# The column step of an inverse 2-D Haar transform: butterflies on VectorE in place of float32r products on TensorE

## The chip, the cores and the metric

The kernel runs on one core of one Trainium2 chip. The metric is the device time of one execution in microseconds; the time of a kernel is the median of its runs. The core's engines each run their own queue of instructions: TensorE (PE; PEld is its weight load), VectorE (DVE), ScalarE (ACT), GpSimd (POOL) and SyncE (SP), which here only issues transfers. PE writes its results to PSUM, which VectorE and ScalarE read.

## The reference

Four layers follow each other on an array of 4 batches, 64 channels and 256 x 256 points, in float32. Layers 0, 1 and 3 are separable 2-D convolutions, written as FFTs, with a residual. Layer 2 is the one in which the change lies: a 2-D Haar transform, two branches that scale the coefficients, mix the channels and shrink the result, and the inverse transform.

```python
def _L2_conv_ref(x, v, conv_w, tau):
    def haar1d_inv(x):
        n = x.shape[-1]
        length = 2
        for _ in range(int(np.log2(n))):
            half = length // 2
            a, d = (x[..., :half], x[..., half:length])
            inter = jnp.stack([NORM * (a + d), NORM * (a - d)], axis=-1)
            inter = inter.reshape(x.shape[:-1] + (length,))
            x = jnp.concatenate([inter, x[..., length:]], axis=-1)
            length *= 2
        return x
...
    f1 = haar2d(x)
    acc = jnp.zeros_like(f1[:, :conv_w.shape[1]])
    for i in range(v.shape[0]):
        f3 = f1 * v[i]
        f4 = jnp.einsum('bchw,oc->bohw', f3, conv_w[i])
        f5 = jnp.sign(f4) * jax.nn.relu(jnp.abs(f4) - tau[i])
        acc = acc + f5
    y = haar2d(acc, inverse=True)
    return y + x
```

Each level of the inverse turns a sum a and a difference d into a + d and a - d, so 8 levels rebuild 256 points from 256 coefficients. The output is layer 3 of this.

## The kernel before

A channel's 256 x 256 points lie as 128 partitions by 512. A convolution of a layer is a product with a Toeplitz matrix along each of the two axes (`contract`, L247 to L251: 128 x 128 weights, 256 and 128 columns, two of each for a product). The Toeplitz tiles are read from DRAM (`toeplitz`, L238). Each batch goes through three stages:

- **Convolutions of layers 0 and 1** (`convolutions`), a channel at a time: products a0, y0, a1, y1, each with a copy or a sum, then the forward Haar transform along the free axis (`pairs` and `levels`, on VectorE and GpSimd) and along the partitions (`down`, a product in two float32r halves). The coefficients go to DRAM as `coef`, and the sums and differences of the first level as `keep`.
- **Mixing** (`mixing`, L404 on), a group of four rows of all channels at a time, 64 groups: the channel product on PE (`mix`, L428), a scaling divided between VectorE (`scaled`, L447) and ScalarE (`scaled_too`, L452), `size` and `sign` on ScalarE (L456, L459), `shrink`, `signed` and `add` on VectorE (L463, L467, L471). `N_ACT` says how many of 16 columns ScalarE scales in each batch. `add` leaves the sum of both branches in the tile z, which holds a whole batch.
- **Inverse** (`inverse`, L491), a channel at a time. `butterfly` (L286, once a batch) makes the coarsest step of one axis. `fetch` loads r, the kept sums and differences, and copies the channel out of z on ScalarE (L501). `rows` (L504) makes one axis by a product with the Haar matrix and a transpose, into the PSUM tile pw. `halves` (L514) splits pw into a float32r part (a cast on ScalarE, L517) and the remainder (L518, VectorE). `cols` (L520) multiplies both halves with the matrix of signs hb, two products into the PSUM tile pu (L524). `join` (L529) adds half of r to pu (L532) and makes the last level (L535, L536), and the result u goes through layer 3: a3, a copy, y3, a sum (L281) and the store.

The order of the work is written out by hand. Every step is an event with a time in ticks, one channel or group per tick, with the offsets of the table `PLACE`; the events are sorted by time and run in that order. Batch b+1's convolutions are spread over batch b's mixing and the start of its inverse, so a mixing shares its ticks with convolutions and most of an inverse has none. In batches 0 to 2 every third channel (`put_off`) leaves layer 3 for later: its u is stored in `late`, and `convolution` takes it up during the last batch's mixing. From these events the build makes each engine's queue and all waits.

Buffers that the steps touch: PSUM tag "mm" has four one-bank tiles, shared by all products but the mixing's; "toep" has 5 tiles, "f" (r and the mixing's coefficients) 3, "mag" 2, "f4" 2, "y" (u among others) 3.

The rows of z are in the order of `_haar_order`, and the tables vt, taut and factors are laid out on the host to suit (`coefficients`, `kernel`).

Of the kernel before, what the change touches and what calls it, by code (L numbers as in the profile page):

```python
# [9 lines left out]
F32 = mybir.dt.float32  # L10
# [7 lines left out]
P = 128  # L18
# [31 lines left out]
    "shrink": 1.777,  # L50
    "signed": 2.802,
    "add": 3.331,
    "fetch": 0.414,
    "rows": 1.071,
    "halves": 1.522,
    "cols": 2.143,
    "join": 2.433,
    "aside": 3.357,
    "a3": 3.47,
    "a3 copy": 3.471,  # L60
    "y3": 4.542,
    "y3 sum": 4.542,
    "out": 5.537,
    "l load": 0.316,
    "l a3": 1.855,
    "l a3 copy": 1.855,
# [29 lines left out]
def conv_seq_kernel(ctx, tc, x, fz, fw, bias, decay, haar, haar_row, factors, vt, taut, wmix, out):  # L96
# [26 lines left out]


    hbt = const.tile([P, P], F32, name="hbt")
    hb = const.tile([P, P], F32R, name="hb")
    hbr = const.tile([P, P], F32R, name="hbr")
    hrow = const.tile([P, 2, P], F32, name="hrow")
    hsinv, ident = hrow[:, 0, :], hrow[:, 1, :]
# [1 line left out]
    bsb = const.tile([P, 3, C], F32, name="bsb")  # L131


    z = zpool.tile([P, 2, S, C], F32, name="z")

    sd = zpool.tile([P, 8, 2, 2, P], F32, name="sd")
    sums = zpool.tile([P, 4, 2, P], F32, name="sums")
# [6 lines left out]

    room = z.rearrange("p h r c -> p (h r c)")
    free = [0]

    def part(n, parts=P):  # L150
        free[0] += n
        return room[:parts, free[0] - n : free[0]]
# [53 lines left out]
        return [load, *steps, end, warm]  # L206

    def constants():
        signs = part(P)
        nc.sync.dma_start(hbt, haar[0])  # L210
        nc.sync.dma_start(signs, haar[1])
        nc.sync.dma_start(hrow, haar_row)
        nc.vector.memset(wb, 0.0)
        for r in range(2):
            nc.sync.dma_start(wb[r * C : (r + 1) * C, r, :], wmix)
        nc.scalar.copy(hb, signs)
        nc.scalar.copy(hbr, hbt)

    def tables():
# [63 lines left out]

        return [product, residual]

    def butterfly(b):  # L286

        d = mx.tile([P, 2, C], F32, name=f"bfly_{b}", tag="mag")
        nc.vector.tensor_sub(d, z[:, :, 0, :], z[:, :, 1, :])
        nc.vector.tensor_add(z[:, :, 0, :], z[:, :, 0, :], z[:, :, 1, :])  # L290
        nc.vector.tensor_copy(z[:, :, 1, :], d)  # L291

# [3 lines left out]
    def at(time, run, unit):  # L298
        events.append((time, len(events), run, unit))
# [104 lines left out]
    def mixing(b, start, n_act):  # L404

        st = {}

        def load(g):
            f = mx.tile([P, 2, S], F32, name=f"f_{b}_{g}", tag="f", bufs=3)
            nc.sync.dma_start(f, coef[b].rearrange("k c p w -> (k c) p w")[:, 2 * g : 2 * g + 2])  # L410
            st[g] = {"f": f}
            if g % GT == 0:
                t = mx.tile([P, 2, GT, 16], F32, name=f"vt_{b}_{g}", tag="vt")
                nc.sync.dma_start(t, scales[g // GT])
                st["vt", g // GT] = t

        def scale(g, i):
            return st["vt", g // GT][:, i, g % GT, :]

        def over(g, i, n):  # L420
            return scale(g, i)[:, :n].unsqueeze(2).to_broadcast([P, n, C])

        def mix(g):
            f = st[g]["f"]
            ps = psx.tile([P, 2, 2, S], F32, name=f"px_{b}_{g}", tag="mix")
            for q in range(2):
                for h in range(2):
                    nc.tensor.matmul(  # L428
                        ps[:, h, q, :],
                        f[:, q, h * P : (h + 1) * P],  # L430
                        wb.rearrange("p r n -> p (r n)"),
                        start=True,
                        stop=True,
                    )
            if g == 0:

                one, two = ps[:, :, 0, :P], ps[:, :, 0, P:]
                d = mx.tile([P, 2, P], F32, name=f"d_{b}", tag="mag")
                nc.vector.tensor_copy(d, two)
                nc.vector.tensor_sub(two, one, d)  # L440
                nc.vector.tensor_add(one, one, d)
            st[g]["f4"] = mx.tile([P, 16, C], F32, name=f"f4_{b}_{g}", tag="f4")
            st[g]["px"] = ps.rearrange("p h q (r i o) -> p (h q r i) o", r=2, i=2)

        def scaled(g):
            px, n = st[g]["px"], 16 - n_act
            nc.vector.tensor_tensor(st[g]["f4"][:, :n], px[:, :n], over(g, 0, n), ALU.mult)  # L447

        def scaled_too(g, half):
            px, f4 = st[g]["px"], st[g]["f4"]  # L450
            for j in range(16 - n_act + half * (n_act // 2), 16 - (1 - half) * (n_act - n_act // 2)):
                nc.scalar.mul(f4[:, j], px[:, j], scale(g, 0)[:, j : j + 1])  # L452

        def size(g):
            mag = st[g]["mag"] = mx.tile([P, 16, C], F32, name=f"mag_{b}_{g}", tag="mag")
            nc.scalar.activation(mag, st[g]["f4"], AF.Abs)  # L456

        def sign(g):
            nc.scalar.activation(st[g]["f4"], st[g]["f4"], AF.Sign)  # L459

        def shrink(g):
            mag = st[g]["mag"]
            nc.vector.tensor_sub(mag, mag, over(g, 1, 16))  # L463

        def signed(g):
            mag = st[g]["mag"]
            nc.vector.scalar_tensor_tensor(mag, mag, 0.0, st[g]["f4"], ALU.max, ALU.mult)  # L467

        def add(g):
            parts = st.pop(g)["mag"].rearrange("p (h r i) o -> p h r i o", h=2, i=2)  # L470
            nc.vector.tensor_add(z[:, :, 4 * g : 4 * g + 4, :], parts[:, :, :, 0, :], parts[:, :, :, 1, :])  # L471

        for g in range(S // 4):
            for name, stage in zip(
                ("mix load", "mix", "scaled", "scaled too", "scaled rest", "size", "sign", "shrink", "signed", "add"),
                (
                    load,
                    mix,
                    scaled,
                    lambda g: scaled_too(g, 0),  # L480
                    lambda g: scaled_too(g, 1),
                    size,
                    sign,
                    shrink,
                    signed,
                    add,
                ),
            ):
                at(start + g + PLACE[name if b + 1 < B else "l " + name], stage, g)

    def inverse(b, start, put_off):  # L491

        st = {}

        def fetch(c):
            if c == 0:
                butterfly(b)
            r = mx.tile([P, 2, 2, P], F32, name=f"r_{b}_{c}", tag="f", bufs=3)
            nc.sync.dma_start(r, keep[b][c])
            a = mx.tile([P, 2, 2, P], F32, name=f"zc_{b}_{c}", tag="mag")  # L500
            nc.scalar.copy(a, z[:, :, :, c].rearrange("p h (i k) -> p h k i", k=2))  # L501
            st[c] = {"r": r, "z": a}

        def rows(c):  # L504
            a = st[c]["z"]
            ps = psm.tile([P, 2, 2, P], F32, name=f"pw_{b}_{c}", tag="mm")
            for m in range(2):
                nc.tensor.matmul(ps[:, 0, m, :], a[:, 0, m, :], hsinv, start=True, stop=True)  # L508
                nc.tensor.transpose(ps[:, 1, m, :], a[:, 1, m, :], ident)  # L509
            st[c]["pw"] = ps  # L510
            if c not in put_off:
                st[c][2] = toeplitz(2, c, f"t2_{b}_{c}")

        def halves(c):  # L514
            w = st[c]["w"] = mx.tile([P, 2, 2, 2, P], F32R, name=f"w_{b}_{c}", tag="f4")
            ps = st[c]["pw"]
            nc.scalar.copy(w[:, 0], ps)  # L517
            nc.vector.tensor_tensor(w[:, 1], ps, w[:, 0].bitcast(F32), ALU.subtract)  # L518

        def cols(c):  # L520
            ps = psm.tile([P, 2, 2, P], F32, name=f"pu_{b}_{c}", tag="mm")
            flat = "p e m w -> p (e m w)"
            for i in range(2):
                nc.tensor.matmul(  # L524
                    ps.rearrange(flat), hb, st[c]["w"][:, i].rearrange(flat), start=(i == 0), stop=(i == 1)
                )
            st[c]["pu"] = ps

        def join(c):  # L529
            ps = st[c]["pu"]  # L530
            t = io.tile([P, 2, 2, P], F32, name=f"t_{b}_{c}", tag="res", bufs=BUFS["res"])
            nc.vector.scalar_tensor_tensor(t, st[c]["r"], 0.5, ps, ALU.mult, ALU.add)  # L532
            u = io.tile([P, 2, S], F32, name=f"u_{b}_{c}", tag="y", bufs=BUFS["y"])
            v = u.rearrange("p m (w e) -> p m w e", e=2)
            nc.vector.tensor_add(v[:, :, :, 0], t[:, 0], t[:, 1])  # L535
            nc.vector.tensor_sub(v[:, :, :, 1], t[:, 0], t[:, 1])  # L536
            st[c]["u"] = u

        def aside(c):
            nc.scalar.dma_start(late[b, c], st.pop(c)["u"])  # L540

        for c in range(C):
            for name, stage in zip(("fetch", "rows", "halves", "cols", "join"), (fetch, rows, halves, cols, join)):
                at(start + c + PLACE[name], stage, c)
            if c in put_off:
                at(start + c + PLACE["aside"], aside, c)
# [171 lines left out]
```

## Time and profile before

| | us |
|---|---|
| three runs | 2941.25 median, 2940.09 to 2941.63 |
| the profiled execution | 2941.06 |
| its span, first to last instruction | 2939.3 |

The granted clock of TensorE is full throughout. The four batches' mixings and inverses lie at 452 to 866 and 866 to 1079 us, 1079 to 1525 and 1525 to 1743, 1743 to 2189 and 2189 to 2403, 2403 to 2688 and 2688 to 2939; before 452 are the filters and batch 0's convolutions. The stage borders are the first and last instructions of `mix`, `add` and `butterfly` in the trace.

Instructions that the change touches, or whose like it adds (mean duration of one from start to write acknowledged; back-to-back instructions of VectorE overlap a little, so the sum of durations exceeds the busy time):

| line | engine, what | count | mean ns |
|---|---|---|---|
| L501 | ACT, copy of a channel out of z, 512 elements with a stride | 256 | 1104 |
| L508, L509 | PE, `rows` | 1024, 512 | 275, 273 |
| L517 | ACT, cast to float32r, 512 elements from PSUM | 256 | 587 |
| L372 | ACT, copy of 512 elements from PSUM | 256 | 683 |
| L532 | DVE, `join`, 512 elements | 256 | 686 |
| L535, L536 | DVE, `join`, 256 elements each | 512 | 418, 421 |
| L471 | DVE, `add`, 512 elements | 256 | 700 |
| L467 | DVE, scalar_tensor_tensor, 1024 elements | 256 | 1223 |
| L289, L290, L291 | DVE, `butterfly`, 128 elements | 4 each | 284, 289, 224 |

Transfers move 649.81 MB, 221 GB/s over the span. In an inverse they are r (256 KB a channel, 3.4 us from issue to landing), the Toeplitz tile of layer 3 (256 KB, 4.0 us) and the result (256 KB, 3.9 us).

To read the views: busy time is the union of an engine's instructions; ends of matmuls are modelled; the idle time in a group's row is that just before its instructions, with what ended it; the chain of waits is followed back from the last instruction and gives each piece the time until the next piece begins.

### The profile page before, as it was taken

The page shows a single profiled execution, that of the slowest core. Times are in us where ns is not written, and L with a number is a line of the kernel's source. Part 1 is how long each engine was busy: PE and PEld are TensorE (multiplying, and loading weights), DVE is VectorE, ACT ScalarE, POOL GpSimd, SP SyncE. Part 2 cuts the span into 40 slices and gives each one's busy share as a digit, 9 for nine tenths or more (in the row PEclk, how much of TensorE's full clock was granted, in tenths as well). Part 3 has the DMA queues.
Part 4 walks back from the last instruction along what each step waited for, and adds up shares of the span by engine and source line. Part 5 has one row for each costly group of instructions (what it writes and reads, how often), then busy time and mean ns, then how long its engine had stood idle before and what let it go on. Part 6 is the DMA issues. An engine that isn't in the chain of part 4 may idle for free. (4 is left out here: it accounts for less than half of the span.)

```text
span 2939.3 us, 52927 instructions
## 1 busy us (share of the span) xinstructions
PE 2894.3 (98%) x16950; PEld 2614.7 (89%) x16950; DVE 2397.6 (82%) x3931; ACT 2179.4 (74%) x5142; POOL 295.5 (10%) x644
## 2 busy tenths in 40 slices
PE   8999999999999999999999999999999999999999
PEld 6899998888888998999998998999998998888998
DVE  4655558988988878999888878999988889998776
ACT  2333348999986768999986768999986768887554
POOL 0111111211110001212110001212110000000000
PEclk9999999999999999999999999999999999999999
DMA  5877787776677876777777876777778878777766
GB/s 160 250 230 230 232 237 216 208 208 200 208 210 245 254 223 199 212 216 210 215 219 242 256 226 198 212 220 210 210 221 245 253 240 236 234 232 218 210 211 187
DMA packets 599368, 649.81 MB, mean 221 GB/s; under 512 B 48465, under 2 KB 517044, under 8 KB 598964
## 3 DMA queue, kind: packets, MB, share of 16 engines
q1 hardware_dynamic: 519860, 562.09, 65.7%
q10 hardware_dynamic: 79232, 84.34, 8.2%
q8 instruction: 137, 2.24, 0.3%
q14 instruction: 139, 1.14, 0.1%
HBM read 426.77 MB, written 219.48 MB: 220 GB/s over the span
## 5 line engine op out<-in xcount | busy, mean ns | idle before, releaser
L250 PE MATMUL py<-t,a 128*128 128x256 f32 x3072 | 920.0, 381 | 7.4 <-ACT a L264 7.0
L264 ACT COPY a<-pa 128x512 f32<-128x512 f32 x768 | 488.9, 637 | 375.2 <-PE pa L251 336.1
L452 ACT ACTIVATE f<-px,vt 128x64 f32<-128x64 f32 x2816 | 621.1, 401 | 94.6 <-DVE f L447 94.5
L251 PEld LDWEIGHTS py<-t,a 128*128 128x128 f32 x3072 | 583.6, 190 | 79.0
L251 PE MATMUL py<-t,a 128*128 128x128 f32 x3072 | 590.2, 274 | 0.0
L250 PEld LDWEIGHTS py<-t,a 128*128 128x128 f32 x3072 | 499.6, 191 | 50.6 <-ACT a L264 17.5
L428 PE MATMUL px<-wb,f 128*128 128x256 f32 x2048 | 489.5, 380 | 6.8 <-ACT f L452 6.7
L428 PEld LDWEIGHTS px<-wb,f 128*128 128x128 f32 x2048 | 369.0, 191 | 49.9 <-ACT f L452 10.0
L330 POOL TENSOR_TENSOR sd<-less 128x128 f32<-128x128 f32 (+4 forms) x320 | 160.3, 501 | 1929.6 <-DVE less L329 1884.5
L353 DVE TENSOR_TENSOR sp<-sd,sp 128x512 fp32r<-128x512 f32 x256 | 182.0, 711 | 184.4 <-ACT sp L348 183.9
L463 DVE TENSOR_TENSOR mag<-mag,vt 128x1024 f32<-128x1024 f32 x256 | 315.0, 1230 | 20.2 <-ACT mag L456 19.2
L467 DVE SCALAR_TENSOR_TENSOR mag<-mag,f 128x1024 f32<-128x1024 f32 x256 | 313.1, 1223 | 6.0 <-ACT f L459 3.8
L456 ACT ACTIVATE mag<-f 128x1024 f32<-128x1024 f32 x256 | 302.1, 1180 | 20.2 <-DVE z L471 19.6
L517 ACT CAST w<-pw 128x512 fp32r<-128x512 f32 x256 | 150.2, 587 | 223.7 <-PE pw L509 214.1
L250 PE MATMUL pa<-t,y 128*128 128x256 f32 x1024 | 307.6, 382 | 7.2 <-DVE y L281 4.1
L250 PE MATMUL pa<-t,x 128*128 128x256 f32 x1024 | 305.9, 381 | 0.4 <-DMA t<-pad 0.4
L459 ACT ACTIVATE f<-f 128x1024 f32<-128x1024 f32 x256 | 289.3, 1130 | 4.4 <-DVE y L281 1.2
L501 ACT COPY zc<-z 128x512 f32<-128x512 f32 x256 | 282.2, 1104 | 4.5 <-DVE z L291 1.4
L281 DVE SCALAR_TENSOR_TENSOR y<-y,bsb,py 128x512 f32<-128x512 f32 x256 | 190.3, 743 | 81.1 <-PE py L251 81.0
L250 PE MATMUL pa<-t,u 128*128 128x256 f32 x772 | 230.2, 380 | 5.3 <-issue 5.3
L532 DVE SCALAR_TENSOR_TENSOR t<-r,pu 128x512 f32<-128x512 f32 x256 | 175.6, 686 | 67.9 <-PE pu L524 64.1
L281 DVE SCALAR_TENSOR_TENSOR y<-x,bsb,py 128x512 f32<-128x512 f32 x256 | 190.3, 743 | 49.2 <-PE py L251 49.0
(72 smaller groups left out, 4636.9 us busy)
## 6 DMA issues: line engine op xcount, KB each, us to landing
t<-pad SPq DMA_DIRECT2D x768, 256.0 KB, 4.0
x<-in_x SPq DMA_DIRECT2D x256, 256.0 KB, 3.7
coef<-co SPq DMA_DIRECT2D x256, 256.0 KB, 3.0
f<-coef SPq DMA_DIRECT2D x256, 256.0 KB, 3.1
r<-keep SPq DMA_DIRECT2D x256, 256.0 KB, 3.4
out_y<-y ACTq DMA_DIRECT2D x256, 256.0 KB, 3.9
keep<-sums SPq DMA_DIRECT2D x256, 128.0 KB, 2.9
keep<-sd SPq DMA_DIRECT2D x256, 128.0 KB, 2.8
```

What stands on the lines that cost most here:

```text
L250: nc.tensor.matmul(ps[:, m, :], src[:, 0, m * P : (m + 1) * P], t[:, ::-1], start=True, stop=False)
L251: nc.tensor.matmul(ps[:, m, P:], src[:, 1, m * P : (m + 1) * P], t[:, : P - 1 : -1], start=False, stop=True)
L264: nc.scalar.copy(a, s["p" + new])
L281: nc.vector.scalar_tensor_tensor(y, s[res], bsb[:, layer, c : c + 1], s["p" + new], ALU.mult, ALU.add)
L353: nc.vector.tensor_tensor(w[:, 1], t, w[:, 0].bitcast(F32), ALU.subtract)
L428: nc.tensor.matmul(ps[:, h, q, :], f[:, q, h * P : (h + 1) * P], wb.rearrange("p r n -> p (r n)"), start=True, stop=True,)
L452: nc.scalar.mul(f4[:, j], px[:, j], scale(g, 0)[:, j : j + 1])
L456: nc.scalar.activation(mag, st[g]["f4"], AF.Abs)
L459: nc.scalar.activation(st[g]["f4"], st[g]["f4"], AF.Sign)
L463: nc.vector.tensor_sub(mag, mag, over(g, 1, 16))
L467: nc.vector.scalar_tensor_tensor(mag, mag, 0.0, st[g]["f4"], ALU.max, ALU.mult)
L501: nc.scalar.copy(a, z[:, :, :, c].rearrange("p h (i k) -> p h k i", k=2))
```

## The change

The levels of the column step are made in z itself, by butterflies on VectorE, before a channel is fetched; the float32r halves, the product with the signs and their tiles and constants go. The layout of z becomes [partition, chunk of 16 channels, row slot, 4, channel in chunk], so that a level of a chunk is one instruction over 64-element runs. `add` becomes two instructions, as the rows it writes go to the slots that in-place butterflies need (`place_of`), and `mix` writes its four results in another order of PSUM banks.

A level n of a chunk is a subtract and a scalar_tensor_tensor on 64n elements; level 32 is in two pieces and level 64 in four. They are placed as follows. Levels 1 to 32 of all four chunks, and level 64 of chunk 0, stand in the batch's own mixing, at ticks 12 to 15 (levels 1 to 8), 22 to 28 (16), 38 to 52 (32) and 43 to 66 (64). Level 64 of chunks 1 to 3 stands in the inverse, four pieces in the 16 ticks before the chunk is fetched. In the last batch all levels of chunks 1 to 3 stand there.

In the inverse `join` reads pw, one step after `rows`; all later steps come one tick sooner. r and the Toeplitz tile are loaded by a step of their own, `early`, ahead of `fetch`.

```diff
+    "early": -0.4,
     "fetch": 0.414,
     "rows": 1.071,
-    "halves": 1.522,
-    "cols": 2.143,
-    "join": 2.433,
-    "aside": 3.357,
-    "a3": 3.47,
...
+    "join": 1.433,
+    "aside": 2.357,
+    "a3": 2.47,
...
+    "level": 0.6,
...
-    z = zpool.tile([P, 2, S, C], F32, name="z")
+    z = zpool.tile([P, 4, P, 4, 16], F32, name="z")
...
+    def halve(even, odd):
+
+        nc.vector.tensor_sub(odd, even, odd)
+        nc.vector.scalar_tensor_tensor(even, even, 2.0, odd, ALU.mult, ALU.subtract)
+
+    def level(n, chunk, begin=0, count=None):
+
+        count = n if count is None else count
+        v = z.rearrange("p n s x c -> p n s (x c)")[:, chunk].rearrange("p (j e s) x -> p j e s x", e=2, s=P // 2 // n)
+        halve(v[:, begin : begin + count, 0, 0, :], v[:, begin : begin + count, 1, 0, :])
+
+    def butterfly():
+
+        v = z.rearrange("p n s (h k) c -> p n s h k c", k=2)
+        for h in range(2):
+            halve(v[:, :, 0, h, 0, :], v[:, :, 0, h, 1, :])
...
-                        ps[:, h, q, :],
+                        ps[:, q, h, :],
...
         def add(g):
-            parts = st.pop(g)["mag"].rearrange("p (h r i) o -> p h r i o", h=2, i=2)
-            nc.vector.tensor_add(z[:, :, 4 * g : 4 * g + 4, :], parts[:, :, :, 0, :], parts[:, :, :, 1, :])
+            parts = st.pop(g)["mag"].rearrange("p (q x i) (n c) -> p q i x n c", q=2, i=2, n=4)
+            for q in range(2):
+                slot = place_of(2 * g + q)
+                nc.vector.tensor_add(
+                    z[:, :, slot].rearrange("p n x c -> p x n c"), parts[:, q, 0], parts[:, q, 1]
+                )
...
+        def early(c):
             r = mx.tile([P, 2, 2, P], F32, name=f"r_{b}_{c}", tag="f", bufs=3)
             nc.sync.dma_start(r, keep[b][c])
+            st[c] = {"r": r}
+            if c not in put_off:
+                st[c][2] = toeplitz(2, c, f"t2_{b}_{c}")
+
+        def fetch(c):
             a = mx.tile([P, 2, 2, P], F32, name=f"zc_{b}_{c}", tag="mag")
-            nc.scalar.copy(a, z[:, :, :, c].rearrange("p h (i k) -> p h k i", k=2))
-            st[c] = {"r": r, "z": a}
+            nc.scalar.copy(a.rearrange("p h k i -> p (h k) i"), z[:, c // 16, :, :, c % 16].rearrange("p i x -> p x i"))
+            st[c]["z"] = a
...
-        def halves(c):
-            w = st[c]["w"] = mx.tile([P, 2, 2, 2, P], F32R, name=f"w_{b}_{c}", tag="f4")
+
+        def join(c):
             ps = st[c]["pw"]
-            nc.scalar.copy(w[:, 0], ps)
-            nc.vector.tensor_tensor(w[:, 1], ps, w[:, 0].bitcast(F32), ALU.subtract)
-
-        def cols(c):
-            ps = psm.tile([P, 2, 2, P], F32, name=f"pu_{b}_{c}", tag="mm")
-            flat = "p e m w -> p (e m w)"
-            for i in range(2):
-                nc.tensor.matmul(
-                    ps.rearrange(flat), hb, st[c]["w"][:, i].rearrange(flat), start=(i == 0), stop=(i == 1)
-                )
-            st[c]["pu"] = ps
-
-        def join(c):
-            ps = st[c]["pu"]
...
+        along = start - groups - 3
+
+        def when(tick, n, chunk, *span):
+            at(tick + PLACE["level"], lambda _: level(n, chunk, *span), 0)
+
+        at(along + 11 + PLACE["level"], lambda _: butterfly(), 0)
+        for chunk in range(4):
+            beside = b + 1 < B or chunk == 0
+            turn = start + 16 * (chunk - 1)
+            for n in (1, 2, 4, 8):
+                when(along + 12 + chunk if beside else turn, n, chunk)
+            when(along + 22 + 2 * chunk if beside else turn + 1, 16, chunk)
+            for i in range(2):
+                when(along + 38 + 4 * chunk + 2 * i if beside else turn + 2 + 2 * i, 32, chunk, 16 * i, 16)
+            for i in range(4):
+                when(turn + 4 + 3 * i if chunk else along + 43 + 8 * i - (i == 3), 64, chunk, 16 * i, 16)
```

## The prediction

> **What bounds the kernel now.** I read the busy table first, then the windows by stage, then the chain of waits, the cost groups and the timeline of one inverse.
>
> ```profile
> PE 2894.3 (98%) x16950; PEld 2614.7 (89%) x16950; DVE 2397.6 (82%) x3931; ACT 2179.4 (74%) x5142; POOL 295.5 (10%) x644
> ```
>
> TensorE is full over the whole span, but the room beside it differs by stage. The windows give span, then busy time of PE, PEld, DVE, ACT and POOL; in order, mixing and inverse of batch 0, of batch 1, and of batch 3 (batch 2 repeats batch 1):
>
> ```profile
> 452.00:866.00 414.00, 407.93 (x2248) 360.72 (x2247) 370.18 (x568) 406.77 (x1229) 75.79 (x130) 1.00 0.69 206
> 866.00:1079.00 213.00, 211.23 (x1350) 193.31 (x1350) 171.26 (x331) 140.24 (x199) 5.42 (x20) 1.00 0.79 242
> 1079.00:1525.00 446.00, 444.50 (x2508) 401.18 (x2507) 398.17 (x610) 399.00 (x1119) 76.15 (x140) 1.00 0.72 211
> 1525.00:1743.00 218.00, 216.23 (x1380) 197.92 (x1380) 174.19 (x336) 143.16 (x205) 5.27 (x20) 1.00 0.79 245
> ...
> 2403.00:2688.00 285.00, 277.01 (x1507) 247.51 (x1505) 278.30 (x330) 243.81 (x574) 0.00 (x0) 1.00 0.79 233
> 2688.00:2939.00 251.00, 246.66 (x1576) 227.35 (x1576) 175.61 (x324) 141.51 (x195) 0.00 (x0) 1.00 0.68 204
> ```
>
> The inverses are TensorE's alone. In the mixings VectorE is close behind (370 of 414, 398 of 446), and in the last one it is the bound: 278.3 of 285, 97.7%. So a microsecond saved on PE counts in the inverses, and one added to VectorE counts in the mixings.
>
> **What the change removes.** Two float32r products per channel (L524), the ScalarE cast (L517) and the VectorE remainder (L518).
>
> ```profile
> L524 PE MATMUL pu<-w,hb 128*128 128x512 f32 x512 | 181.4, 435 | 0.0
> L518 DVE TENSOR_TENSOR w<-pw,w 128x512 fp32r<-128x512 f32 x256 | 175.3, 685 | 2.5 <-ACT w L517 2.5
> L463 DVE TENSOR_TENSOR mag<-mag,vt 128x1024 f32<-128x1024 f32 x256 | 315.0, 1230 | 20.2 <-ACT mag L456 19.2
> ```
>
> The chain of waits (start, length, what) prices them better, because it counts each step only until the next begins:
>
> ```profile
> 2854.11 0.46 PE pu L524 x2
> ...
> 2632.28 1.13 DVE mag L463
> 2633.93 1.22 DVE mag L467
> ```
>
> The pair of products holds the path for 0.46 us: 256 x 0.465 = 119 us, about 30 in each inverse. The Trainium skill, Perfetto Trace Analysis, section Identifying the Most-Contended Engine, calls matmul busy time a bad measure because matmuls are pipelined. The busy row would make the gain 181 us and the end 62 us lower than the chain does; the chain agrees with the page, so the chain is used.
>
> On ScalarE 37.5 us go from each inverse, where it has 70 us free: worth nothing. On VectorE L518 goes: 64 x 0.60 (its start to L535's in the timeline below) = 38.5 us per inverse.
>
> **What it adds to VectorE.** A butterfly is a subtract and a scalar_tensor_tensor that waits for it. Level n of a chunk is 64n elements: 64, 128, 256, 512, then 1024 once, twice and four times. For 1024 elements the chain shows 1.13 followed by independent work and 1.22 followed by a wait: 2.35 a pair, 7 pairs a chunk, 16.5 us. The small levels by rows: 0.69 (L518), 0.42 (L535), 0.28 (L289), and about 0.22 for 64 elements, which no row has (an estimate, 0.28 less half the step from 0.42); twice their sum is 3.2. A chunk is 19.7 us, 16 of them 315 us. `add` becomes two instructions of 256 elements, 0.33 apart, for one of 512 at 0.60: +0.07 x 64 = 4.5 us per mixing. The old butterfly (three instructions, 0.8 us) and the new (four) cancel.
>
> The Trainium skill, VectorE: DVE Perf Modes, section The DRAIN you can't avoid, speaks against the change: the next instruction starts only when the pipe is empty, and chained ones gain nothing. The rows show an independent successor starting 0.1 us before the reported end (1.13 against 1.23). By the rule a pair would be 2.46 and all levels 12 us dearer; the rows are used.
>
> By stage, in us of VectorE: mixing 0 to 2 get levels 1 to 32 of four chunks, 4 x (3.2 + 3 x 2.35) = 41.0, level 64 of chunk 0, 9.4, and 4.5: **+55 each**. Mixing 3 gets one chunk and 4.5: **+24**. Inverses 0 to 2: -38.5 + 12 x 2.35 = **-10**. Inverse 3: -38.5 + 59 = **+21**.
>
> **Where that lands.** Mixing demand becomes 425, 453, 453 and 302 us. If every idle moment were used the stages grow by 11, 7, 7 and 17, together 42; if the added work overlapped nothing, by 189. The nearest row is mixing 3, which VectorE bounds at 97.7%; dividing by that gives 435, 464, 464 and 309: +21, +18, +18, +24 = **+81**, which I take.
>
> The inverses lose 119 on PE and must hand some back, because VectorE's levels come between steps that PE needs. Its queue there, batch 3:
>
> ```profile
> 2748.67 0.75 DVE L281 SCALAR_TENSOR_TENSOR y<-u,bsb,py 128x512 f32<-128x512 f32 x1 [0.66 <-PE py L251]
> 2749.80 0.69 DVE L532 SCALAR_TENSOR_TENSOR t<-r,pu 128x512 f32<-128x512 f32 x1 [0.38 <-PE pu L524]
> 2750.41 0.68 DVE L518 TENSOR_TENSOR w<-pw,w 128x512 fp32r<-128x512 f32 x1
> 2751.01 0.42 DVE L535 TENSOR_TENSOR u<-t 128x256 f32<-128x256 f32 x1
> 2751.34 0.42 DVE L536 TENSOR_TENSOR u<-t 128x256 f32<-128x256 f32 x1
> 2752.42 0.75 DVE L281 SCALAR_TENSOR_TENSOR y<-u,bsb,py 128x512 f32<-128x512 f32 x1 [0.66 <-PE py L251]
> ```
>
> A tick is 3.74 us and becomes 3.28: a3 1.31, y3 1.31, rows 0.66. VectorE does the y3 sum (0.66) and `join` (about 1.39 with its wait) and idles 1.2 us, room for one 1024-element instruction per tick. Written in the order of the code, a pair of 2.35 stands between a y3 sum and the `join` behind it, and a3 waits for that `join`. It has 3.94 us (rows, a3, y3, rows) for 2.25, so a pair makes PE 0.8 late; the five crowded ticks at a chunk's start cost about 6, the three later pairs 2.4, some 9 us a chunk, 28 for batch 3. In batches 0 to 2 every third channel is put off, three ticks take PE 7.2 and the window is 2.63 us: 2.1 late per pair in chunks 1 and 3, about 0.8 in chunk 2, 20 per batch. That is the upper end, 88; the lower is 0.
>
> The queue is not the order of the code, though: L518 stands between the instructions of one `join` above, and the cast of `constants`, placed at tick 4.93 (about 42 us by the `pairs` instructions, which place tick 4.64 at 40.4), ran at once:
>
> ```profile
> L217 ACT CAST hbr<-hbt x1: 298/298/298, 8.2 to 8.2; 128x128 fp32r<-128x128 f32 x1
> ```
>
> So the build moves ready work forward into idle time, and levels are ready long before they are due. I take three tenths of the upper end: 6, 6, 6 and 8, **+26**.
>
> **At nothing**, with cover: `early` issues r 0.8 and the t2 load 1.5 ticks sooner on SP; r's third-last buffer is free 1.2 ticks before, so nothing behind it (coefficient, x and filter loads) waits; if it were not, `join` would be late by part of a 3.4 us landing. PSUM has one allocation per channel less. The channel copy (L501, 1.10 us) reads with another stride; between 0.68 (L372) and 2.2 (twice its row) ScalarE stays under 175 of 183 us. The new bank order of `mix` lets L447 start up to 0.43 us sooner; VectorE waits for px 9.5 us in mixing 0, so 0 to -9.5; I take 0. DMA moves the same bytes in about 189 instead of 213 us: 242 GB/s becomes 273, which single slices of 4 us in the inverse of batch 0 exceed:
>
> ```profile
> GB/s 256 190 267 219 312 226 253 311 212 311 192 310 244 245 258 224 250 277 281 229 284 207 326 266 228 259 221 261 242 268 212 273 217 236 262 251 259 226 242 243
> ```
>
> **Sum**, on the profiled execution (2941.06 us: span 2939.3 and 1.8 around it; the runs' median is 2941.25, the same): 2941 - 119 + 81 + 26 = **2929 us**.
>
> **Rivals.** (1) VectorE's idle takes it all: +42 in the mixings, nothing handed back: 2864; with half of each expected loss, about 2885. For it: levels wait for nobody and fit any gap. Against: three engines at 98% in mixing 0 have never run without waits. Chance 0.18. (2) Slower: the level pairs stand where the code puts them, between the y3 sum and `join`, and PE waits at a3: +88 in the inverses, 2941 - 119 + 81 + 88 = 2991. It decides from 38 us handed back. For it: VectorE's own work per chunk in inverse 3 (16 x 2.05 + 19.7 = 52.5) equals PE's (16 x 3.28 = 52.5). Against: the moved instructions above. Chance 0.33. (3) The change doesn't do what it says because the transfers hold the first three inverses at their length: -22 from inverse 3 and +81 give 3000. For it: DMA is busy 0.79 there already; against: the slices at 310 GB/s. Chance 0.05.
>
> **How the numbers follow.** The forecast has 0.44, its own range 2905 to 2947. A measurement here tells about 0.2% from no change, 2935.4 to 2947.1. Faster is 0.30 of the forecast's 0.44 and rival 1: 0.48; same 0.10; slower 0.04 of the forecast and rivals 2 and 3: 0.42. The range 2880 to 3005 leaves out nearly half of rival 1 and the far parts of rivals 2 and 3, together 0.2.
>
> **What would show it.** Mixings of 435, 464, 464 and 309 us with VectorE at 97%; inverses of about 190, 194, 190 and 229 us, each with some 6 us in which a3 waits for `join`; L524's 119 us gone from PE. If the first mixing stays below 425 the levels were cheaper than 2.35 a pair; if PE shows over 15 us of waits for `join` in an inverse, rival 2 holds; if r lands late, rival 3.

## The result, and the profile after

| | before | after |
|---|---|---|
| median of five runs, us | 2941.25 | 2954.99 |
| lowest to highest | 2939.57 to 2941.98 | 2952.87 to 2959.32 |
| profiled span, us | 2939.3 | 2957.5 |

The ratio is 1.0049, 95% interval 1.0034 to 1.0064: the changed kernel is slower by half a per cent, more than the 0.2% that a measurement here can tell. The forecast was 2929 us, faster. It missed by 26 us and had the wrong sign. The profiled execution is the slowest of the five.

The busy table of the kernel after:

```profile
PE 2826.3 (96%) x16438; PEld 2541.0 (86%) x16438; DVE 2529.3 (86%) x4287; ACT 2056.6 (70%) x4885; POOL 361.2 (12%) x644
```

The 512 products are gone (16950 to 16438) and the butterflies are there: VectorE is busy 132 us longer. Yet the span is 18 us longer, and TensorE, full before, now stands idle. The windows by stage of the kernel after say where (span, then busy time of PE, PEld, DVE, ACT, POOL, the granted clock, the DMA share and GB/s); mixing and inverse of batches 0, 1 and 3:

```profile
451.00:884.00 433.00, 418.26 (x2284) 367.20 (x2283) 421.53 (x709) 410.11 (x1233) 80.84 (x130) 1.00 0.67 200
884.00:1096.00 212.00, 188.99 (x1194) 172.22 (x1193) 158.45 (x288) 108.76 (x133) 12.90 (x20) 0.96 0.77 242
1096.00:1550.00 454.00, 452.25 (x2544) 407.19 (x2543) 443.36 (x741) 398.34 (x1121) 95.23 (x140) 1.00 0.71 209
1550.00:1767.00 217.00, 196.06 (x1221) 177.76 (x1220) 162.06 (x295) 111.57 (x138) 12.71 (x20) 0.95 0.78 242
...
2429.00:2733.00 304.00, 285.28 (x1517) 250.94 (x1515) 300.00 (x422) 248.02 (x575) 0.00 (x0) 0.99 0.74 220
2733.00:2957.00 224.00, 216.35 (x1432) 200.94 (x1432) 185.07 (x318) 108.39 (x129) 0.00 (x0) 1.00 0.75 224
```

With the stage borders put at the first product of `mix` and the first copy of `fetch` in both traces:

| stage | before | after | difference | predicted |
|---|---|---|---|---|
| mixings 0 to 3 | 415.6, 447.8, 447.8, 287.2 | 433.3, 454.0, 453.9, 303.9 | +18, +6, +6, +17 | +21, +18, +18, +24 |
| inverses 0 to 2 | 211.1, 217.0, 211.9 | 211.9, 216.8, 208.5 | +1, 0, -3 | -24 each |
| inverse 3 | 250.9 | 224.3 | -27 | -22 |

The mixings grew less than predicted and inverse 3 shrank more. But inverses 0 to 2 lost 30 us of products each and are as long as before: all of the error is there. TensorE is busy 189 of 212 us in inverse 0, against 211 of 213 before.

Cut into its start, its middle and its end, inverse 0 of the kernel after (the same view):

```profile
884.00:932.00 48.00, 37.62 (x199) 33.41 (x198) 45.29 (x69) 16.37 (x23) 12.54 (x18) 0.86 0.56 170
932.00:1024.00 92.00, 81.14 (x520) 73.28 (x520) 61.15 (x118) 52.48 (x66) 0.36 (x3) 0.98 0.80 250
1024.00:1096.00 72.00, 70.23 (x478) 65.53 (x478) 52.01 (x103) 39.91 (x46) 0.00 (x0) 1.00 0.89 280
```

There are two places, and they differ. In the first 48 us VectorE is full (45.3) and TensorE idles 10 us. In the next 92 VectorE has 31 us free and TensorE still idles 11. At the end nothing waits, and the transfers run at 280 GB/s.

The start, on VectorE and then on TensorE (the timeline of the kernel after: start, length, line, operation, shape, and in brackets the idle time before it and what ended it). Lines are numbered as in the changed kernel: L284 and L285 are the two instructions of a pair of a level, L533, L536 and L537 are `join`, L246 and L247 the products of `contract`, L277 the sum behind a y product, and L322, L323 and L359 belong to the next batch's convolutions.

```profile
889.94 1.21 DVE L284 TENSOR_TENSOR z<-z 128x1024 f32<-128x1024 f32 x1
891.08 0.41 DVE L322 TENSOR_TENSOR sums<-y 128x256 f32<-128x256 f32 x1
891.41 0.42 DVE L323 TENSOR_TENSOR sd<-y 128x256 f32<-128x256 f32 x1
891.75 1.21 DVE L285 SCALAR_TENSOR_TENSOR z<-z 128x1024 f32<-128x1024 f32 x1
892.89 0.68 DVE L533 SCALAR_TENSOR_TENSOR t<-r,pw 128x512 f32<-128x512 f32 x1
895.11 0.69 DVE L359 TENSOR_TENSOR sp<-sd,sp 128x512 fp32r<-128x512 f32 x1 [1.55 <-ACT sp L354]
895.72 0.42 DVE L536 TENSOR_TENSOR u<-t 128x256 f32<-128x256 f32 x1
896.06 0.42 DVE L537 TENSOR_TENSOR u<-t 128x256 f32<-128x256 f32 x1
```

```profile
893.78 0.38 PE L247 MATMUL py<-t,a 128*128 128x128 f32 x2
896.53 0.73 PE L246 MATMUL pa<-t,u 128*128 128x256 f32 x2 [2.37 <-DVE u L537]
```

Levels stand here that the code places as late as tick 45 of the inverse: the build moved them forward, as it moved the cast of `constants`, and all 12 pairs of level 64 of chunks 1 to 3 are done by 931 us, when channel 6 has just come to `join`. One `join` is drawn out over 3.6 us, because work of the next batch's last convolutions (L359, which waits 1.55 us for ScalarE) stands in it, and a3 waits 2.37 us.

The middle holds no level at all. What the y3 sums waited for there (the view of one line, idle time of its engine and what ended it):

```profile
L277 DVE SCALAR_TENSOR_TENSOR y<-u,bsb,py x38: 737/747/749, 907.0 to 1076.9; 128x512 f32<-128x512 f32 x38
...
  PE py L247: 22.9, 17
  DMA coef<-co: 8.6, 6
```

And one such wait, on VectorE:

```profile
961.06 0.69 DVE L533 SCALAR_TENSOR_TENSOR t<-r,pw 128x512 f32<-128x512 f32 x1
963.12 0.75 DVE L277 SCALAR_TENSOR_TENSOR y<-u,bsb,py 128x512 f32<-128x512 f32 x1 [1.37 <-DMA coef<-co]
963.78 0.42 DVE L536 TENSOR_TENSOR u<-t 128x256 f32<-128x256 f32 x1
964.12 0.42 DVE L537 TENSOR_TENSOR u<-t 128x256 f32<-128x256 f32 x1
```

```profile
964.64 0.67 PE L246 MATMUL pa<-t,u 128*128 128x256 f32 x2 [1.35 <-issue]
```

The sum writes into a tile of tag "co", of which there are two. The coefficient copies of the next batch's last convolutions (L378) use the same two, and a tile is free only when its store has landed, 3.2 us (coefficients) or 3.8 us (results) after its issue. So the sum waits for a store, VectorE's queue stands behind it, `join` is late, and a3 begins 0.1 us after `join` ends.

### The profile page after: what moved, and what is told of

Same layout as the page of the kernel before. It is cut to its first block, busy times and chain, and to the rows that moved or that the text cites. A ratio compares the mean times of both kernels' runs of the same rounds, so it can differ in the third digit from the quotient of the medians.

```text
span 2957.5 us, 52078 instructions
## 1 busy us (share of the span) xinstructions
PE 2826.3 (96%) x16438; PEld 2541.0 (86%) x16438; DVE 2529.3 (86%) x4287; ACT 2056.6 (70%) x4885; POOL 361.2 (12%) x644
## 5 line engine op out<-in xcount | busy, mean ns | idle before, releaser
L246 PE MATMUL py<-t,a 128*128 128x256 f32 x3072 | 927.7, 384 | 8.8 <-ACT a L260 8.3
L247 PEld LDWEIGHTS py<-t,a 128*128 128x128 f32 x3072 | 587.6, 191 | 81.3
L247 PE MATMUL py<-t,a 128*128 128x128 f32 x3072 | 593.3, 275 | 0.0
L246 PEld LDWEIGHTS py<-t,a 128*128 128x128 f32 x3072 | 498.2, 193 | 48.3 <-ACT a L260 19.6
L336 POOL TENSOR_TENSOR sd<-less 128x128 f32<-128x128 f32 (+4 forms) x320 | 200.8, 627 | 1899.8 <-DVE less L335 1644.8
L246 PE MATMUL pa<-t,y 128*128 128x256 f32 x1024 | 310.3, 385 | 16.6 <-DVE y L277 10.0
L246 PE MATMUL pa<-t,x 128*128 128x256 f32 x1024 | 305.8, 380 | 0.9 <-issue 0.9
L246 PE MATMUL pa<-t,u 128*128 128x256 f32 x772 | 241.0, 395 | 61.4 <-issue 42.6
L359 DVE TENSOR_TENSOR sp<-sd,sp 128x512 fp32r<-128x512 f32 x256 | 178.1, 696 | 128.0 <-ACT sp L354 126.5
L277 DVE SCALAR_TENSOR_TENSOR y<-u,bsb,py 128x512 f32<-128x512 f32 x193 | 143.7, 745 | 144.9 <-PE py L247 108.9
L277 DVE SCALAR_TENSOR_TENSOR y<-x,bsb,py 128x512 f32<-128x512 f32 x256 | 189.3, 740 | 46.7 <-PE py L247 45.7
L247 PEld LDWEIGHTS pa<-t,y 128*128 128x128 f32 x1024 | 195.6, 191 | 26.8
L247 PEld LDWEIGHTS pa<-t,x 128*128 128x128 f32 x1024 | 194.6, 190 | 26.3
```

The lines of the kernel that those rows point to most:

```text
L246: nc.tensor.matmul(ps[:, m, :], src[:, 0, m * P : (m + 1) * P], t[:, ::-1], start=True, stop=False)
L247: nc.tensor.matmul(ps[:, m, P:], src[:, 1, m * P : (m + 1) * P], t[:, : P - 1 : -1], start=False, stop=True)
L277: nc.vector.scalar_tensor_tensor(y, s[res], bsb[:, layer, c : c + 1], s["p" + new], ALU.mult, ALU.add)
L336: engine.tensor_tensor(t[:, :, :, half:length], v[..., 0], v[..., 1], ALU.subtract)
```

## The experiments

All twelve are variants of the changed kernel, but for one of the kernel before. Ratios are to the kernel before on the same chip; its medians on the chips used lie within 2.3 us of each other.

**Four kernels: buffers against levels.** Theory: the "co" buffers hold the middle, the level instructions the start. Rival: it is the levels alone, as rival 2 had it.

Four "co" buffers in place of two:

```diff
-BUFS = {"res": 1, "y": 3, "co": 2}
+BUFS = {"res": 1, "y": 3, "co": 4}
```

> The changed kernel with four buffers for the tag co (the results of layer 3 and the coefficients) instead of two; 2954.99 us with two. Theory (the y3 sum waits for a buffer whose store has not landed, holds VectorE's queue, and with it join and a3): from channel 6 to 36 of inverses 0 to 2 a tick falls from about 3.1 us to 2.55, some 16 us a batch; in all about 2907 us, and the waits of the y3 sum on a transfer are gone. Rival one (the transfers of these stretches are too slow): no change, within 5 us. Rival two (the Haar levels on VectorE make the waits): no change in those channels, since no level runs there.

Measured: 2917.06 us, ratio 0.9908 [0.9893, 0.9923]. This one number turns the loss into a gain of 0.9%. Its y3 sums (the same view of one line) wait for no transfer any more:

```profile
L277 DVE SCALAR_TENSOR_TENSOR y<-u,bsb,py x41: 734/745/750, 907.5 to 1077.2; 128x512 f32<-128x512 f32 x41
...
  PE py L247: 22.9, 20
  ACT a L260: 1.2, 1
```

Inverses 0 to 2 take 198.0, 199.8 and 196.5 us; the other stages moved by less than 1 us. Start, middle and end of inverse 0:

```profile
885.00:933.00 48.00, 38.55 (x208) 34.03 (x206) 45.49 (x69) 16.93 (x23) 12.92 (x20) 0.86 0.56 173
933.00:1024.00 91.00, 89.33 (x590) 81.88 (x591) 69.39 (x137) 59.68 (x74) 0.00 (x0) 1.00 0.93 287
1024.00:1083.00 59.00, 58.17 (x398) 54.59 (x397) 42.15 (x83) 31.92 (x37) 0.00 (x0) 1.00 0.92 286
```

TensorE is full in the middle; the start is as it was. The gain is 10 us short of the 2907 expected.

The kernel before with four buffers, as a control:

> The kernel before with four buffers for co. Theory: its inverse has waits of 1.9 us on PE in all, so the buffer costs it nothing: 2941 us, within 4. Rival (more buffers help any kernel of this layout): 2 us or more faster per batch, below 2933 us.

Measured: 2943.08 us, ratio 0.9999 [0.999, 1.0008]. Two buffers were enough at its tick of 3.0 us in the middle of these inverses; they are not at the 2.65 us to which the tick falls with four.

Level 64 of chunks 1 to 3 left out in batches 0 to 2:

```diff
-            for i in range(4):
+            for i in range(4 if b + 1 == B or chunk == 0 else 0):
```

> The changed kernel without level 64 of chunks 1 to 3 in batches 0 to 2 (24 instructions of 1024 elements per batch left out), two buffers for co. Theory of the buffer: only the first 48 us of each of the three inverses get shorter, by 10 to 15 us a batch, and channels 6 to 36 stay at about 3.1 us a tick: 2910 to 2925 us. Rival (the levels are all of it): the 30 us of waits in each inverse go, about 2860 us.

Measured: 2925.40 us, ratio 0.9936 [0.992, 0.9952], just above what was expected. `join` of channel 12 comes 6 to 12 us sooner, counted from the first fetch copy; channels 12 to 36 still take 3.1 to 3.2 us each on average, against 3.1 to 3.3 with these levels. So these levels are not what holds the middle.

All levels left out:

```diff
-        nc.vector.tensor_sub(odd, even, odd)
-        nc.vector.scalar_tensor_tensor(even, even, 2.0, odd, ALU.mult, ALU.subtract)
+        return
```

> The changed kernel without any level and without butterfly (all added VectorE work except the second add left out). Theory: the mixings return to 414, 448, 448 and 287 us (48 us less), the starts of the inverses lose 12 us each and inverse 3 some 5; channels 6 to 36 keep their 3.1 us a tick. About 2955 - 48 - 41 = 2866 us. Rival (the levels are all of it): PE's 119 us come out whole, 2941 - 119 = 2822 us.

Measured: 2887.23 us, ratio 0.9799 [0.978, 0.9819], above both expectations. The middle of inverse 0 in this kernel:

```profile
932.00:1024.00 92.00, 80.73 (x521) 73.58 (x522) 61.25 (x120) 51.26 (x62) 0.00 (x0) 0.98 0.80 246
```

Without any level TensorE loses the same 11 of 92 us there. In the middle rival 2 falls and the buffers stand.

**Four more: how many buffers, what the levels cost, and what the build's order is worth.** Three buffers:

> The changed kernel with three buffers for co (two: 2954.99 us, four: 2917.06). Theory: a y3 sum comes some 2 to 2.4 us behind the last one where no channel is put off between, and a coefficient tile takes a buffer for about 5 us (copy 0.7, store 3.9) every fourth tick; with three buffers the third-last store has had 5 us or more, so nearly all of the wait goes: 2917 to 2925 us. Rival (what counts is the room for coefficients of several channels at once): halfway, about 2936 us.

Measured: 2915.41 us, ratio 0.9908 [0.9893, 0.9923]: the third buffer does it all, the fourth nothing.

No levels and four buffers:

> Four buffers for co and no levels and no butterfly (left out). Theory: the two causes stand at different places (channels 6 to 36 against mixings and starts of inverses) and add up: 2917 less the 68 us that leaving out the levels brought with two buffers, 2849 us. Rival (they wait for the same thing): above 2865 us.

Measured: 2841.95 us, ratio 0.9658 [0.9642, 0.9674], 7 below. This closes a table of medians in us:

| | levels | no levels | levels cost |
|---|---|---|---|
| two co buffers | 2955.0 | 2887.2 | 68 |
| four co buffers | 2917.1 | 2842.0 | 75 |
| two instead of four cost | 38 | 45 | |

The two costs are almost independent. And 2842 is 20 above 2941 - 119 = 2822: with neither cost, a sixth of the gain on TensorE still doesn't arrive. The start of inverse 0 in this kernel, and the whole of it:

```profile
883.00:931.00 48.00, 45.23 (x296) 41.25 (x295) 34.70 (x69) 26.38 (x33) 2.85 (x10) 1.00 0.86 262
866.00:1056.00 190.00, 185.00 (x1224) 170.39 (x1223) 139.41 (x272) 110.72 (x137) 5.87 (x20) 1.00 0.90 275
```

Without levels TensorE is busy 45.2 us of these 48, against 38.6 with four buffers and the levels: in inverse 0 the levels hold the start.

The pairs of level 64 held back to the tick where the code has them, by a one-element multiply on ScalarE that each pair must wait for (four buffers):

```diff
+        def hold(c, chunk, begin):
+            odd = z[:, chunk, 2 * begin + 1, 0, 0:1]
+            nc.scalar.mul(junk, odd, st[c]["z"][:, 0, 0, 0:1])
...
+                if chunk and b + 1 < B:
+                    c = 16 * (chunk - 1) + 4 + 3 * i
+                    at(start + c + 0.45, lambda _, c=c, chunk=chunk, i=i: hold(c, chunk, 16 * i), 0)
```

> Four buffers for co, and each pair of level 64 of chunks 1 to 3 in batches 0 to 2 held back to the tick where the code puts it, by a one-element ScalarE multiplication that reads its data and the fetched channel of that tick. The starts of the inverses lose 22 of 28 us of VectorE work and get shorter by 10 to 12 us each. Theory of the prediction's second rival (a pair between a y3 sum and join makes PE 0.8 to 2.1 us late): 12 pairs hand back 15 to 20 us a batch, so 2930 to 2940 us in all. Rival (VectorE is at 60% there and the pairs hide): about 2885 us.

Measured: 2928.00 us, ratio 0.9949 [0.9934, 0.9964], 11 above the kernel with four buffers. Inverses 0 to 2 take 201.8, 210.8 and 205.4 us, each 12 to 13 more than without levels; rival 2 had priced such pairs at 20. So rival 2's mechanism is real. By moving the pairs forward the build avoids 24 of these 37 us in the inverses; as it puts some of them into the mixings, and mixings 0 to 2 are 3 to 4 us longer each, 11 are left as its gain by the medians.

Two more columns of the last batch's scaling on ScalarE, to ease VectorE in mixing 3 (four buffers):

```diff
-N_ACT = (14, 12, 12, 6)
+N_ACT = (14, 12, 12, 8)
```

> Four buffers for co, and in the last batch's mixing ScalarE scales 8 of 16 columns instead of 6, so VectorE's scaling falls by 128 elements, 0.13 us a group, 8.5 us in all, and ScalarE's grows by 0.42 us a group (248 to 275 us of about 303). Theory (VectorE bounds the last mixing): 2908 to 2910 us. Rival (ScalarE's scaling, for which PE waits, bounds it too): 2917 us or more.

Measured: 2925.17 us, ratio 0.994 [0.9925, 0.9954]: the theory falls, and the rival's number holds. Mixing 3 with 6 columns, and then, in the kernel with 8:

```profile
2388.00:2691.00 303.00, 282.95 (x1512) 249.31 (x1510) 299.82 (x423) 248.66 (x575) 0.00 (x0) 1.00 0.75 221
```

```profile
2388.00:2701.00 313.00, 289.70 (x1513) 251.69 (x1512) 308.00 (x443) 269.62 (x703) 0.00 (x0) 0.98 0.74 214
```

VectorE's freed time was filled: it runs 20 instructions more, 11 of them level instructions of 1024 elements (25 in place of 14) that the build now moves forward into this stage, and inverse 3 gained next to nothing from their absence (223.6 us against 224.3). VectorE is busy 308 of that stage's 313 us. ScalarE has a part in it too: TensorE's waits for its copy a, before y3, rise from 4.3 to 12.9 us. Which of the two made the stage longer isn't separated.

**The starts.** Four kernels, all with four buffers. Idle products in the first ten ticks of inverses 0 to 2, which keep TensorE busy and are read by nobody:

```diff
+        def filler(c):
+            ps = psx.tile([P, 2, S], F32, name=f"fill_{b}_{c}", tag="mix")
+            for i in range(3):
+                nc.tensor.matmul(ps[:, i % 2, :], hrow[:, 0, :], hrow.rearrange("p e w -> p (e w)"), start=True, stop=True)
...
+            if b + 1 < B and c < 10:
+                at(start + c + 0.6, filler, c)
```

> Four buffers for co (2917.06 us), and three idle float32 products of 256 columns (about 1.3 us, results unused) on PE in each of the first ten ticks of inverses 0 to 2, 39 us of PE in all. The clock of PE fell to 0.5 in nine places of the profile with four buffers, 31 us in all, seven of them in or just ahead of these starts; in the kernel before in none. Theory (the clock falls because PE waits): with the waits filled the steps in the starts are gone, which is worth up to half of their length, some 10 us, against fillers that stand in the way: 2907 to 2920 us, granted clock 0.999. Rival (the clock falls for another reason): the steps stay and the fillers cost 20 us or more, 2937 us.

Measured: 2914.65 us, ratio 0.9905 [0.989, 0.9919], 2 below the kernel without them, with overlapping intervals. The first start of this kernel, to be read against the row 885 to 933 above:

```profile
886.00:934.00 48.00, 46.78 (x281) 41.78 (x280) 46.45 (x74) 19.70 (x26) 13.43 (x20) 1.00 0.67 197
```

The clock stays whole (1.00 against 0.86), 39 us of added products cost nothing, and nothing clear of noise is won either: TensorE was not what the start waits for.

Level 64 of chunks 1 to 3 in pieces of 512 elements in place of 1024:

```diff
-                when(turn + 4 + 3 * i if chunk else along + 43 + 8 * i - (i == 3), 64, chunk, 16 * i, 16)
+                tick = turn + 4 + 3 * i if chunk else along + 43 + 8 * i - (i == 3)
+                for half in range(2 if chunk and b + 1 < B else 1):
+                    n = 8 if chunk and b + 1 < B else 16
+                    when(tick, 64, chunk, 16 * i + 8 * half, n)
```

> Four buffers for co, and level 64 of chunks 1 to 3 in batches 0 to 2 in eight pieces of 512 elements in place of four of 1024 (0.60 against 1.14 us for an instruction, 3 us more per batch). Theory one (a level instruction that has begun blocks VectorE for 1.1 us while join waits): the starts of the inverses get 3 to 6 us shorter each, 2900 to 2908 us. Theory two (the starts are long because VectorE is full there, whatever the pieces): 2917 to 2926 us.

Measured: 2905.36 us, ratio 0.9872 [0.9856, 0.9889], the best of those that leave nothing out, though VectorE does more instructions for the same levels. Its first start:

```profile
885.00:933.00 48.00, 41.81 (x255) 37.44 (x254) 43.86 (x86) 21.98 (x30) 11.15 (x20) 0.96 0.71 212
```

TensorE gets 3.3 us more done, and mixings 1 and 2 are 2.5 us shorter each. But the profiled execution, at 2912.9, is the slowest of its four, and inverses 1 and 2 are no shorter in it. That shorter instructions block less fits the first start; where the rest of the 12 us comes from isn't shown.

The loads of r and of the Toeplitz matrices at their old places (`early` emptied, its loads back in `fetch` and `rows`):

> Four buffers for co, and the loads of r and of the Toeplitz tile of layer 3 where they were before the change: r with fetch, the tile with rows. Theory (the build issues them as soon as a buffer is free, wherever the code has them): 2917 us within 4. Rival (the earlier place is part of what keeps the fast ticks at 2.41 us): 2925 us or more, and join waits for r.

Measured: 2911.88 us, ratio 0.9896 [0.9881, 0.9911], 5 below with overlapping intervals. `early` brings nothing; whether it costs a little stays open.

All together, pieces, idle products and old places:

> The changed kernel with four co buffers, level 64 of chunks 1 to 3 in eight pieces of 512 elements, three idle products in each of the first ten ticks of inverses 0 to 2, and the loads of r and of the Toeplitz matrices at their old places. Theory one (the separate gains are of different causes and add up): from the 2905 us of the kernel with the pieces, less the 2 to 3 us of the idle products and the 5 us of the old places, 2896 to 2902 us. Rival (the pieces already took away the waits whose halved clock the idle products avoid, and the old places were worth nothing beyond the scatter): 2903 to 2909 us.

Measured: 2916.98 us, ratio 0.991 [0.9894, 0.9927]. Both theories fall: the pieces' gain is gone. Its first start:

```profile
881.50:929.50 48.00, 44.93 (x264) 40.62 (x263) 43.90 (x85) 18.52 (x25) 9.72 (x20) 0.96 0.62 190
```

TensorE is busy 44.9 us, 13 us of each inverse with idle products, and `join` of channel 12 comes 64, 70 and 69 us after the first fetch copy of inverses 0 to 2, against 56, 64 and 66 with the pieces alone. A likely reading is that idle products which cost nothing beside long waits stand in the way once the waits are short; no run has the pieces with one of the two other edits alone.

## Why the prediction was wrong

**The products: right in the last inverse, a little high over the whole.** The removed pair was worth what the chain said, not what the busy row said. Inverse 3's tick is 3.29 us (predicted 3.28), and without levels and with four buffers that stage is 30.5 us shorter (predicted 30). Over the whole of that kernel TensorE is busy 110 us less than before (2784.0 against 2894.3), not 119 and not 181.

**The levels: close in sum, in part by luck.** The prediction had them cost 81 us in the mixings and part of 26 in the inverses. Measured with four buffers: 75, of which 58 in the mixings (18, 11, 11, 17) and 17 in the inverses (8, 2, 3, 4). With two buffers the mixings grew by 47 us in place of 81.

In mixings 1 and 2 the mechanism was another. VectorE runs at 443.4 of 454 us there, the 97.7% by which the prediction divided, but TensorE runs at 452.3, and it was full before too. These stages grew by 6 us because they hold 28 of TensorE's instructions more, which the inverses' starts no longer hold. The 11 us against the kernel without levels are 51 such instructions in the same way. So it is a shift of the border that made these two stages longer, and not VectorE's ceiling.

VectorE's demand was also counted too high: mixings 0, 1 and 3 got 51, 45 and 22 us of its busy time, where 55, 55 and 24 were counted. A pair, counted at 2.35 us with a wait in it, mostly has none, since in 109 of 112 pairs other work stands between L284 and L285: in the median each holds the queue for 1.14 us, 2.27 a pair. That is 1 to 2 us a mixing; the small levels, counted by whole durations, are some 3 more. The rest is overlap of the other work: counted from start to start, VectorE's other instructions take 392 us in mixing 1 with four buffers, and 398 there in the kernel without levels. The Trainium skill, VectorE: DVE Perf Modes, section The DRAIN you can't avoid, has the next instruction wait until the pipe is empty, and lets one that is not held start earlier; here the successor starts 0.07 us before the reported end of 1.21, so the rows served better.

**The failed step: "three tenths of the upper end: 6, 6, 6 and 8, +26".** The inverses handed back 31, 30, 26 and 3 us, together 90 of the 119. With the mixings' 47 that is the profiled execution: 2941 - 119 + 47 + 90 = 2959. The prediction looked for one reason only, levels between a y3 sum and `join`. There were three, here by the stages of the profiled executions:

- the "co" buffers: 43 us (38 by the medians), shown by three and by four of them, and by the kernel without levels
- levels in the inverses: 17 us with four buffers, but in inverses 0 to 2 not where rival 2 had them; the build puts them into the starts, where VectorE then is full
- some 30 us that remain without levels and with four buffers. The mixings of that kernel are together 10 us shorter than before, so 20 are left in all. Of these, 9 are TensorE's busy time, which fell by 110 and not by 119 us, and 11 its idle time: 4.6 to 5.0 us in each of inverses 0 to 2, against 1.8 before, and some 2 in mixing 3. What holds these was not tried.

The first belongs to the paragraph "At nothing". It named r's buffers, PSUM, SP's order and the DMA rate, each with its cover, and not the buffers of the y3 result. Two numbers that were at hand pointed there: a store's landing of 3.9 us, and a tick that falls from 3.0 to 2.6 us while the coefficient tiles of the next batch pass through the same two buffers.

The mean of the tick alone would not have shown it. In the kernel with four buffers, between `join` of channel 6 and of channel 36 of inverse 0, a tile is held for 5.2 us in the median, from the first write to the landing of its store, where the trace tells the landing. The next use but one of the pool, which with two buffers needs the same tile, begins 5.7 us later on average, but in 7 of 26 cases only 2.5 to 3.0 us later. In the kernel before the tile was held for 4.9 us, and that use never came sooner than 5.1. The third use behind, which needs the tile with three buffers, comes after 7.7 us at the least.

**The rivals.** Rival 1's floor of +42 in the mixings was nearly reached (+47), its "nothing handed back" not at all. Rival 2 had named 15 us of waits in an inverse as its mark, and the trace shows 18 to 22 us of TensorE's idle time before a3 in inverses 0 to 2. But the mark tells where TensorE waits, not who holds `join`: without any level the waits of the middle are as long. Held to the code's places the pairs cost 12 to 13 us an inverse, where it had 20. That price is a little high by its own terms: 2.25 + 2.35 - 3.94 makes a pair 0.7 us late and not 0.8, and 2.0 and not 2.1 in the narrow window. Rival 1's 2885 would be 2876 with half of 81 and half of 26. Rival 3 falls: the ends of the inverses move 280 GB/s, and 287 in the middle with four buffers.

**The moved transfers** (`early`) were costed at nothing; the run with them moved back is no slower.

## What to carry to other kernels

When an edit shortens a loop's tick, go through every buffer pool of the loop, results too, and ask who else takes from it: the shortest time from one use to the use that needs the same buffer, and not the mean, must exceed the time from first write to the end of the store. A third buffer was worth 40 us here, three times what the change as made had lost. A build that moves ready work forward filled the idle time that an edit freed, so an added load is priced at the place where it becomes ready, not only where the code puts it.

## What the hardware showed unexpectedly

TensorE's granted clock fell to one half after waits as short as 1.88 us. Before, it was whole to the end; after, it was halved in 12 places before the last microseconds, 48 us in all. It changes on a grid of 3.41 us. Three windows of that grid in a row in the kernel after (the columns as in the windows by stage):

```profile
907.31:910.72 3.41, 1.65 (x13) 1.36 (x11) 3.41 (x6) 1.37 (x2) 0.00 (x0) 1.00 0.70 212
910.73:914.14 3.41, 1.45 (x9) 1.35 (x10) 3.41 (x6) 0.00 (x0) 0.00 (x0) 1.00 0.86 203
914.14:917.55 3.41, 3.41 (x15) 3.05 (x14) 3.32 (x6) 0.58 (x1) 0.00 (x0) 0.50 0.57 202
```

The idle time of the first two is one wait of 3.73 us, which the border of the grid cuts. After a window with 1.76 us of it the clock stays whole; after one with 1.96 us it is halved for a window, and then it comes back. The shortest wait that was followed by half clock lay within one window, which ended at 808.33 us (TensorE's timeline):

```profile
807.21 1.13 PE L434 MATMUL px<-wb,f 128*128 128x256 f32 x4 [1.88 <-ACT f L458]
```

In eleven traces, those of the kernel after and of ten variants that show such steps, I took all windows at whole clock between 450 and 2800 us: those idle for 1.88 us or more were followed by half clock, those idle for 1.87 us or less were not, with one exception (1.97 us, in the kernel with all edits together). The longest wait that had no effect lasted 2.82 us, in the kernel without level 64, and the grid cut it into 1.05 and 1.77. The Trainium skill, TensorE: Matmul & The Clock Gate, section What's actually happening, asks for at least one idle window of about 3.4 us. The length of the window agrees; a little more than half of it idle was enough here.

What the halved clock costs seems small in this kernel: where idle products kept it whole, in the starts, the time fell by 2 us, which the runs can't tell from nothing. What the idle products themselves cost is in that number too.
